# A decoder layer on one core: the cross attention's mask moves from TensorE products to a VectorE add, with norms and self values in other slots

## The chip, the core and the metric

The kernel runs on one core of one Trainium2 chip. The metric is the time of one execution in device microseconds (us); the figure for a kernel is the median of its runs. Five engines work beside each other: TensorE (PE in the profile: matrix products, with its weight loads shown apart as PEld), VectorE (DVE), ScalarE (ACT), GpSimd (POOL) and SyncE (SP, which here only issues DMAs).

## What is computed

One decoder layer with norms after each residual sum, for 32 sequences of 256 tokens, 256 features, float32 in and out. Cut to what matters:

```python
x = layernorm(x + self_attention(x))        # 16 heads of 64, 4 kv heads, rotary, ALiBi bias
x = layernorm(x + cross_attention(x, ctx))  # 16 heads of 16, windows of 64 tokens
x = layernorm(x + ffn(x))                   # 256 -> 1024 (gate, up) -> 256, quantized weights
# inside cross_attention, per head:
p = einsum(q, k) / sqrt(16)
p = where(mask, p, finfo.min)               # causal, own and previous window, same cell id
a = softmax(p); o = einsum(a, v)
```

The cross attention's mask depends on the token's cell id, so it is made anew for every sequence; all 16 heads share it.

## The kernel before, in words

**Tiles and stages.** One sequence (a "batch" b) is the unit. Its 256 query tokens are two tiles of 128. Self attention is cut into 8 units of a batch (a query tile, a pair of kv heads and two of their groups: four heads), cross attention into 4 units (a query tile and 8 of 16 heads: two halves of four heads each). A unit's scores go to two PSUM banks of 128x512 float32 (one "half" each).

**Order.** TensorE, VectorE and ScalarE run in an order written out by hand: the loop at the end of the kernel goes through slots, two to a step, and emits the instructions of each slot one function after the other. GpSimd and SyncE are placed by the framework's scheduler. Each engine works through its own queue in order. In step n (part 0, then part 1):

- part 0: `self_turn(n-1)` transposes the probabilities of the unit before (L452, into bank t, copied to pT by ScalarE, L457); then the cross attention's pieces, then `self_scores(n)`: products (L396), ALiBi product (L406), row maximum by VectorE (nm, L417), exponentials by ScalarE (p, L423).
- part 1: `self_normal(n)` scales p by the reciprocal row sums on VectorE (rinv L437, p L440); in even steps `self_values` multiplies pT with v (L469) and ScalarE copies the result (oT, L476).
- in odd steps `cross_mask` (part 0, ahead of the self scores) and `cross_scores` (after them) run, in part 1 the exponentials of the first half; the second half's exponentials, the transposes of the cross probabilities (xt, L688), the values (xo, L704) and the transposing back (xr, L724) follow in the next two steps.
- the rest are generators, which do one piece in a slot and then `yield` the number of slots to the next: `self_inputs` (projections, L333, of the next batch), `self_output` (wo, L484), `cross_inputs` (norm of the context zc, its transposes zcT, keys L594, values L606, the mask's tile), `cross_output` (norm of the attention output zo, transposes zoT, product xw L750, residual sum L754, norm of x2) and `feed_forward` (ff L797, gu L812 and L818, ffm L824, gu L833 on GpSimd, hib L836, hiT L843, ffo L849).

**Cross scores before.** `cross_mask` takes two banks (`xs`) and starts each with one bfloat16 product of an identity with the mask tile, repeated over four heads (L643, 128x512): so the bank holds 0 or a large negative number. `cross_scores` accumulates the scores onto it (L657), VectorE takes the row maxima from the bank (xnm, L666), and ScalarE computes the exponentials out of the bank into the SBUF tile xp (L679). The two banks stay taken from the mask product until the last exponential. All eight PSUM banks come from one pool.

**Norms.** A norm is: statistics on VectorE (L180, L181), reciprocal root on GpSimd in three small operations (`rstd_of`, L187 to L189), scaling on ScalarE (`scaled`, L201). Where the scaling stands in a list named `last`, it is emitted when that list is emptied: ahead of the self scores in part 0, and at the end of a slot.

**Eight steps are one period**: in steady state one batch enters and one leaves in 8 steps. I number them 0 to 7: step 0 is the one of a batch's first self unit. Cross scores fall in steps 1, 3, 5 and 7, self values in 0, 2, 4 and 6.

Of the kernel before, what the change touches and what calls it, by code (L numbers as in the profile page):

```python
# [10 lines left out]
BF16 = mybir.dt.bfloat16  # L11
# [39 lines left out]
def kernel(  # L51
# [159 lines left out]
    def prepare_cross():  # L211


        nc.sync.dma_start(vecs_sb, vecs)
        nc.sync.dma_start(cols_sb, cols)
        for j, (w, dst) in enumerate(
            (
                (wxk, xkv_w[:, :, 0:D]),
                (wxv, xkv_w[:, :, D : 2 * D]),
                (wxq, xq_w),  # L220
                (wxo, xo_w),
            )
        ):
            raw = work("tr", [P, NDC, D], 3)
            nc.sync.dma_start(raw, w.rearrange("(c p) n -> p c n", p=P))
            for dc in range(NDC):
                nc.gpsimd.tensor_scalar(
                    dst[:, dc, :], raw[:, dc, :], vecs_sb[:, j, 0, dc : dc + 1], None, ALU.mult
                )
            if j == 0:  # L230
                nc.sync.dma_start(wo_sb, Wo.rearrange("(c p) n -> p c n", p=P))
            if j in xbias:
                more = work("xp", [P, 512])
                row = more[:, 0:D]
                nc.sync.dma_start(row, rows[j].partition_broadcast(P))
                for dc in range(NDC):
                    nc.gpsimd.tensor_scalar(
                        more[:, D + dc * P : D + (dc + 1) * P],
                        ones,
                        vecs_sb[:, j, 1, dc : dc + 1],  # L240
                        None,
                        ALU.mult,
                    )
            yield 2
            pb = bank("mm")
            if j in xbias:
                for dc in range(NDC):
                    nc.tensor.matmul(
                        pb[:, 0:D],
                        more[:, D + dc * P : D + (dc + 1) * P],  # L250
                        raw[:, dc, :],
                        start=(dc == 0),
                        stop=(dc == NDC - 1),
                    )
                nc.vector.tensor_tensor(xbias[j], pb[:, 0:D], row, ALU.add)
            else:
                for ch in range(NDC):
                    for dc in range(NDC):
                        nc.tensor.matmul(
                            pb[:, ch : ch + 1],  # L260
                            raw[:, dc, ch * P : (ch + 1) * P],
                            vecs_sb[:, j, 1, dc : dc + 1],
                            start=(dc == 0),
                            stop=(dc == NDC - 1),
                        )
                nc.vector.tensor_tensor(xbcol[j], pb[:, 0:NDC], cols_sb[:, j, :], ALU.add)
            yield 2
# [291 lines left out]
    def cross_inputs(b):  # L559
# [12 lines left out]
            last.append(partial(scaled, zc[:, t, :], cs[:, t, :], rstds[t]))  # L572
        ck = work("ck", [P, L], 1)
        nc.gpsimd.tensor_copy(ck, ck_i)
        yield
        zcT = work("tr", [P, NDC, L], 3)
        for t in range(NT):
            transposed(zcT[:, :, t * P : (t + 1) * P], zc[:, t, :], "zcT")


        eq = work("eq", [P, NT, P], 1)
        s["mask"] = mask = work("mask", [P, NT, P], 2, BF16)
        for rows_, t, k0 in ((slice(0, P), 0, 0), (slice(0, 64), 1, 64), (slice(64, P), 1, 128)):
            nc.gpsimd.tensor_scalar(
                eq[rows_, t, :], ck[rows_, k0 : k0 + P], cq_sb[rows_, b, t : t + 1], BIG, ALU.is_equal, ALU.mult
# [49 lines left out]

    spans = {0: ((0, P, 0, 0),), 1: ((0, 64, 64, NT), (64, P, P, 1))}

    def cross_mask(b, i):
        s = state[b]
        qc, ch = cross_units[i]  # L640
        s["xs", i] = banks = [bank("xs") for _ in range(2)]
        for half in range(2):
            nc.tensor.matmul(  # L643
                banks[half].rearrange("p (h k) -> p h k", k=P),
                ident_b,
                s["mask"][:, qc, :].unsqueeze(1).to_broadcast([P, XHH, P]),
                start=True,
                stop=False,
            )

    def cross_scores(b, i):
        s = state[b]
        qc, ch = cross_units[i]
        for q0, q1, k0, _t in spans[qc]:
            for half in range(2):
                rows_ = slice(half * 64, (half + 1) * 64)
                nc.tensor.matmul(  # L657
                    s["xs", i][half].rearrange("p (h k) -> p h k", k=P)[q0:q1],
                    s["xqT", qc][rows_, ch, q0:q1],
                    kTz[rows_, ch, :, k0 : k0 + P],  # L660
                    start=False,
                    stop=True,
                )
        s["xnm", i] = [small("xnm", 4) for half in range(2)]
        for half in range(2):
            nc.vector.tensor_reduce(  # L666
                s["xnm", i][half],
                s["xs", i][half].rearrange("p (h k) -> p h k", k=P),
                AX.X,
                ALU.max,  # L670
                negate=True,
            )

    def cross_exp(b, i, half):
        s = state[b]
        s["xp", i, half] = p = work("xp", [P, 512])
        for j in range(XHH):
            cols = slice(j * P, (j + 1) * P)
            nc.scalar.activation(  # L679
                p[:, cols], s["xs", i][half][:, cols], AF.Exp, bias=s["xnm", i][half][:, j : j + 1]  # L680
            )

    def cross_turn(b, i, half):
# [53 lines left out]
    def cross_output(b, t):  # L737
        s = state[b]
        on = s["on", t]
        mv = stats(on, "zo")  # L740
        rstd = rstd_of(mv, "zo")
        yield
        last.append(partial(scaled, on, on, rstd))
        yield 2
        zoT = work("zT", [P, NDC, P])
        transposed(zoT, on, "zoT")
        yield
        py = bank("xw")
        for dc in range(NDC):
            nc.tensor.matmul(py[:, 0:D], zoT[:, dc, :], xo_w[:, dc, :], start=(dc == 0), stop=(dc == NDC - 1))  # L750
        if t == 0:
            s["x2"] = work("x2", [P, NT, D])
        h = s["x2"][:, t, :]
        nc.vector.tensor_tensor(h, py[:, 0:D], s["x1", t], ALU.add)  # L754
        mv = stats(h, "x2")
        rstd = rstd_of(mv, "x2")
        yield
        scaled(h, h, rstd)


    def feed_forward(b):
# [112 lines left out]
    for b in range(B):  # L874
        s0 = 16 * b
        if b:
            at(s0 - 16, self_inputs(b))
        at(s0 + 3, cross_inputs(b))
        for t in range(NT):
            at(s0 + 2 * (5 + 4 * t), self_output(b, t))  # L880
            at(s0 + 2 * (CROSS + 5 + 4 * t) + 1, cross_output(b, t))
        at(s0 + 2 * (CROSS + 11) + 2, feed_forward(b))

    with tc.manual_schedule(engines={mybir.EngineType.PE, mybir.EngineType.DVE, mybir.EngineType.Activation}):
        running = []
        slot = min(starts)
        while starts or running:
            step, part = divmod(slot, 2)
            k, odd = divmod(step - CROSS, 2)
            for gen in starts.pop(slot, ()):  # L890
                running.append([slot, gen])

            def cross(f, unit, *more):
                if 0 <= unit < 4 * B:
                    f(*divmod(unit, 4), *more)

            def own(f, unit):
                if 0 <= unit < 8 * B:
                    f(*divmod(unit, 8))


            if part == 1:
                own(self_normal, step)
            if part == 1 and not odd:
                cross(cross_exp, k, 0)
            if part == 0 and odd:
                cross(cross_exp, k, 1)
            for r in list(running):
                if r[0] == slot:
                    wait = next(r[1], r)  # L910
                    if wait is r:
                        running.remove(r)
                    else:
                        r[0] += wait or 1
            if part == 0:
                own(self_turn, step - 1)
                if odd:
                    cross(cross_back, k - 1)
                    cross(cross_turn, k, 0)
                else:  # L920
                    cross(cross_turn, k - 1, 1)
                    cross(cross_mask, k)
                flush()
                own(self_scores, step)
                if not odd:
                    cross(cross_scores, k)
            else:
                if step % 2 == 0 and 0 <= step // 2 - 1 < 4 * B:
                    self_values(*divmod(step // 2 - 1, 4))
                if not odd:  # L930
                    cross(cross_values, k - 1)
            flush()
            slot += 1
# [95 lines left out]
```

## Time and profile before

| What | us |
|---|---|
| median of three runs (lowest, highest) | 2486.79 (2483.45, 2487.99) |
| the profiled execution | 2485.1 |
| its span, from the first to the last instruction | 2483.3 |
| TensorE busy in the span | 2362.9 |
| VectorE busy | 1947.5 |
| ScalarE busy | 1710.2 |
| GpSimd busy | 1117.4 |

The profile is of one execution. It gives for each group of instructions (a line of the kernel, an engine, the tiles written and read) the count, the busy time, the mean duration in ns, and the idle time of the engine just ahead of it with what ended it. The timeline lists instructions in order of time. "In 74.07 us a batch" below is the distance at which the timeline repeats itself: the transposes zoT ahead of a step 0 start at 1202.57 and at 1276.64 on TensorE.

### The profile page before, as it was taken

What the parts mean: (1) busy time and instruction counts of PE and PEld (TensorE: products, weight loads), DVE (VectorE), ACT (ScalarE), POOL (GpSimd) and SP (SyncE); (2) the same over time, 40 slices, a digit from 0 to 9 for tenths busy, and PEclk for the clock granted to TensorE, in tenths of its full rate; (3) what the DMA queues carried; (4) which work ended last, traced back from release to release, by engine and by line L of the source; (5) the groups of instructions that cost most, each with busy time, mean ns of one, the idle gap of its engine ahead of it and who ended that gap; (6) DMA issues with size and microseconds to landing.
All of it is one profiled execution on the core that took longest, in us unless ns stands there. A gap on an engine that the chain in (4) does not pass through costs nothing.

```text
span 2483.3 us, 52717 instructions
## 1 busy us (share of the span) xinstructions
PE 2362.9 (95%) x17956; PEld 1689.6 (68%) x17956; DVE 1947.5 (78%) x4773; ACT 1710.2 (69%) x5057; POOL 1117.4 (45%) x1855
## 2 busy tenths in 40 slices
PE   6999999999999999999999999999999999999985
PEld 4766776776777666777666777676776666777653
DVE  4867877877777887877887878887887887878865
ACT  2566766766767766767766767766767766767763
POOL 6244444444444444444444444444444444444432
PEclk9999999999999999999999999999999999999996
DMA  5211211111111121121111121111211111111000
GB/s 177 79 46 44 53 51 46 41 45 48 52 53 46 35 50 48 50 54 46 36 49 48 52 53 46 37 49 48 52 52 46 36 50 46 51 48 37 22 21 9
DMA packets 104824, 121.09 MB, mean 49 GB/s; under 512 B 21734, under 2 KB 74854, under 8 KB 104556
## 3 DMA queue, kind: packets, MB, share of 16 engines
q1 hardware_dynamic: 103424, 115.96, 17.6%
q8 instruction: 143, 2.34, 0.4%
q10 hardware_dynamic: 1132, 1.76, 0.2%
q14 instruction: 125, 1.02, 0.1%
HBM read 37.69 MB, written 8.39 MB: 19 GB/s over the span
## 4 chain that ended last, share of the span: by engine, by line
PE 63%; DVE 17%; POOL 7%; ACT 7%; DMA 3%; issue 2%; SPq 1%; POOLq 0%; ACTq 0%; DVEq 0%
PE proj L333 10%; PE s L396 9%; PE t L452 6%; PE o L469 5%; PE wo L484 5%; DVE p L440 4%; ACT p L423 4%; DVE nm L417 3%; PE xs L657 3%; PE xt L688 3%; PE ff L797 3%; PE xv L606 2%; PE xk L594 2%; PE v L365 2%; DVE gu L812 2%
## 5 line engine op out<-in xcount | busy, mean ns | idle before, releaser
L423 ACT ACTIVATE p<-s,nm 128x256 f32<-128x256 f32 x1024 | 471.8, 474 | 190.4 <-DVE nm L417 188.1
L417 DVE TENSOR_REDUCE nm<-s 128x2 f32<-128x512 f32 x512 | 329.0, 684 | 189.0 <-PE s L406 170.3
L440 DVE TENSOR_SCALAR p<-p,rinv 128x256 f32<-128x256 f32 x1024 | 454.0, 485 | 18.1
L457 ACT COPY pT<-t 128x512 f32<-128x512 f32 x512 | 285.3, 629 | 84.4 <-PE t L452 80.6
L396 PE MATMUL s<-kT,qT 64*128 64x256 f32 x2048 | 313.4, 406 | 6.8 <-DVE gu L812 6.3
L679 ACT ACTIVATE xp<-xs,xnm 128x128 f32<-128x128 f32 x1024 | 303.0, 416 | 5.2 <-DVE xnm L666 5.2
L452 PE MATMUL t<-ident,p 128*128 128x128 f32 x2048 | 272.5, 275 | 8.1 <-DVE p L440 7.7
L452 PEld LDWEIGHTS t<-ident,p 128*128 128x128 f32 x2048 | 236.1, 141 | 34.4 <-DVE p L440 5.7
L396 PEld LDWEIGHTS s<-kT,qT 64*128 64x128 f32 x2048 | 186.2, 187 | 105.5 <-DVE gu L812 29.1
L333 PE MATMUL proj<-xT,wq_sb 128*128 128x256 f32 x1024 | 254.7, 392 | 0.0
L469 PE MATMUL o<-pT,v 128*64 128x256 f32 x2048 | 252.7, 389 | 0.0
L484 PE MATMUL wo<-wo_sb,oT 128*128 128x256 f32 x1024 | 250.2, 387 | 0.0
L357 POOL TENSOR_TENSOR qT<-qT,other 128x512 f32<-128x512 f32 x128 | 164.6, 1286 | 184.5 <-DMA other<-psin 143.7
L484 PEld LDWEIGHTS wo<-wo_sb,oT 128*128 128x128 f32 x1024 | 190.3, 191 | 60.1 <-issue 36.6
L333 PEld LDWEIGHTS proj<-xT,wq_sb 128*128 128x128 f32 x1024 | 185.8, 191 | 46.3 <-issue 25.7
L555 POOL TENSOR_TENSOR qb<-qb,rx_sb 128x256 f32<-128x256 f32 (+1 forms) x96 | 87.3, 910 | 275.5 <-DMA other<-qb 266.7
L423 ACT ACTIVATION_READ_ACCUMULATOR p<-s,nm 128x1 f32 x1024 | 210.1, 205 | 0.0
L469 PEld LDWEIGHTS o<-pT,v 128*64 128x64 f32 x2048 | 136.8, 138 | 89.1 <-issue 24.1
L201 ACT ACTIVATE x<-x,rstd_x 128x256 f32<-128x256 f32 x64 | 38.3, 598 | 194.6 <-DVE ffm L824 177.3
L666 DVE TENSOR_REDUCE xnm<-xs 128x4 f32<-128x512 f32 x256 | 163.8, 681 | 3.4 <-PE xs L657 3.4
L690 ACT COPY xpT<-xt 128x512 f32<-128x512 f32 x256 | 164.0, 641 | 1.4 <-ACT pT L457 0.3
L342 DVE TENSOR_TENSOR psin<-proj,rs_sb 128x512 f32<-128x512 f32 x160 | 110.6, 691 | 55.6 <-PE proj L333 49.8
(159 smaller groups left out, 4646.7 us busy)
## 6 DMA issues: line engine op xcount, KB each, us to landing
other<-psin SPq DMA_DIRECT2D x640, 64.0 KB, 2.0
xT<-in_xt_dram SPq DMA_DIRECT2D x32, 256.0 KB, 2.8
xs<-in_x_dram SPq DMA_DIRECT2D x32, 256.0 KB, 2.8
cs<-in_ctx_dram SPq DMA_DIRECT2D x32, 256.0 KB, 2.9
other<-qb SPq DMA_DIRECT2D x64, 128.0 KB, 2.0
kTz<-tr SPq DMA_DIRECT2D x256, 32.0 KB, 2.0
other<-qb SPq DMA_DIRECT2D x128, 64.0 KB, 1.9
out_dram<-y SPq DMA_DIRECT2D x32, 256.0 KB, 2.3
```

The costliest lines, as they stand in the source:

```text
L333: nc.tensor.matmul(pq[:, c * L : (c + 1) * L], w[:, dc, c * P : (c + 1) * P], xT[:, dc, :], start=(dc == 0), stop=(dc == NDC - 1),)
L357: nc.gpsimd.tensor_tensor(d2, d2, other, ALU.add)
L396: nc.tensor.matmul(banks[half][:, rr * L : (rr + 1) * L], qT[rows_, rr, qc * P : (qc + 1) * P], kT[rows_, kc, :], start=(rr == 0), stop=False,
L417: nc.vector.tensor_reduce(nm, banks[half].rearrange("p (h k) -> p h k", k=L), AX.X, ALU.max, negate=True)
L423: nc.scalar.activation(p[:, cols], banks[half][:, cols], AF.Exp, bias=nm[:, rr : rr + 1], accum_out=sums[:, rr : rr + 1],)
L440: nc.vector.tensor_scalar(p[:, cols], p[:, cols], rinv[:, rr : rr + 1], None, ALU.mult)
L452: nc.tensor.transpose(pt[:, j * P : (j + 1) * P], p[half][:, rr * L + kk * P : rr * L + (kk + 1) * P], ident,)
L457: nc.scalar.copy(pT[half], pt)
L469: nc.tensor.matmul(po[half * HD : (half + 1) * HD, rp * L : (rp + 1) * L], s["v"][:, kk, (2 * kc + half) * HD : (2 * kc + half + 1) * HD], ...
L484: nc.tensor.matmul(py[:, 0:D], s["oT", qc, kc][:, r, :], wo_sb[:, 4 * kc + r, :], start=(kc == 0 and r == 0), stop=(kc == 1 and r == 3),)
L679: nc.scalar.activation(p[:, cols], s["xs", i][half][:, cols], AF.Exp, bias=s["xnm", i][half][:, j : j + 1])
L690: nc.scalar.copy(pT, pt)
```

## The change

Three things are changed.

1. `cross_mask` and its two products are gone. `cross_scores` takes its banks after the self scores, its products start the banks themselves (`start=True`), and VectorE then adds the mask (now float32 instead of bfloat16) to each bank and writes the sum to the SBUF tile xp. Row maxima are taken from xp, and the exponentials work in place in xp. xp has 4 buffers instead of 2.
2. Norms' slots: `cross_inputs` starts one slot earlier and waits one slot more between its scaling and its transposes; in `cross_output` the transposes and all after them come one slot earlier, and the last scaling goes into `last`, so that it stands at the end of its slot.
3. `self_values` moves from part 1 of an even step, where it stood behind the generators' pieces, to part 0, directly behind the self scores.

```diff
@@ prepare_cross
-                more = work("xp", [P, 512])
+                more = work("xp", [P, 512], 4)
@@ cross_inputs (its start: at(s0 + 3, ...) becomes at(s0 + 2, ...))
         nc.gpsimd.tensor_copy(ck, ck_i)
-        yield
+        yield 2
         zcT = work("tr", [P, NDC, L], 3)
...
-        s["mask"] = mask = work("mask", [P, NT, P], 2, BF16)
+        s["mask"] = mask = work("mask", [P, NT, P])
@@
-    def cross_mask(b, i):
-        s = state[b]
-        qc, ch = cross_units[i]
-        s["xs", i] = banks = [bank("xs") for _ in range(2)]
-        for half in range(2):
-            nc.tensor.matmul(
-                banks[half].rearrange("p (h k) -> p h k", k=P),
-                ident_b,
-                s["mask"][:, qc, :].unsqueeze(1).to_broadcast([P, XHH, P]),
-                start=True,
-                stop=False,
-            )
-
     def cross_scores(b, i):
         s = state[b]
         qc, ch = cross_units[i]
+        banks = [bank("xs") for _ in range(2)]
         for q0, q1, k0, _t in spans[qc]:
...
-                    start=False,
+                    start=True,
                     stop=True,
                 )
+        for half in range(2):
+            s["xp", i, half] = p = work("xp", [P, 512], 4)
+            nc.vector.tensor_tensor(
+                p.rearrange("p (h k) -> p h k", k=P),
+                banks[half].rearrange("p (h k) -> p h k", k=P),
+                s["mask"][:, qc, :].unsqueeze(1).to_broadcast([P, XHH, P]),
+                ALU.add,
+            )
         s["xnm", i] = [small("xnm", 4) for half in range(2)]
         for half in range(2):
             nc.vector.tensor_reduce(
                 s["xnm", i][half],
-                s["xs", i][half].rearrange("p (h k) -> p h k", k=P),
+                s["xp", i, half].rearrange("p (h k) -> p h k", k=P),
@@ cross_exp
-        s["xp", i, half] = p = work("xp", [P, 512])
+        p = s["xp", i, half]
...
-                p[:, cols], s["xs", i][half][:, cols], AF.Exp, bias=s["xnm", i][half][:, j : j + 1]
+                p[:, cols], p[:, cols], AF.Exp, bias=s["xnm", i][half][:, j : j + 1]
@@ cross_output
         last.append(partial(scaled, on, on, rstd))
-        yield 2
+        yield
         zoT = work("zT", [P, NDC, P])
...
-        scaled(h, h, rstd)
+        last.append(partial(scaled, h, h, rstd))
@@ the loop over the slots
                     cross(cross_turn, k - 1, 1)
-                    cross(cross_mask, k)
                 flush()
                 own(self_scores, step)
                 if not odd:
                     cross(cross_scores, k)
-            else:
                 if step % 2 == 0 and 0 <= step // 2 - 1 < 4 * B:
                     self_values(*divmod(step // 2 - 1, 4))
+            else:
                 if not odd:
                     cross(cross_values, k - 1)
```

In the changed program's written order, the statistics of zc stand in VectorE's queue ahead of step 3's nm (they stood at that step's end), the product xw stands in TensorE's queue ahead of the next step's transposes t (it stood behind the next step's self scores), and on GpSimd the reciprocal root of the first x2 tile stands ahead of the rotation of the cross queries (qb, other, xqT, L555 to L557). On SyncE the load of the cell ids stands behind the copies into kTz and the copies of qb instead of ahead of them.

More of the change, by code (lines that the diff above doesn't have):

```diff
@@ L657, in cross_scores @@
                 nc.tensor.matmul(
-                    s["xs", i][half].rearrange("p (h k) -> p h k", k=P)[q0:q1],
+                    banks[half].rearrange("p (h k) -> p h k", k=P)[q0:q1],
                     s["xqT", qc][rows_, ch, q0:q1],
                     kTz[rows_, ch, :, k0 : k0 + P],
-                    start=False,
+                    start=True,
                     stop=True,
                 )
+        for half in range(2):
[6 more added lines that the diff above has]
+            )
         s["xnm", i] = [small("xnm", 4) for half in range(2)]
@@ L877 @@
             at(s0 - 16, self_inputs(b))
-        at(s0 + 3, cross_inputs(b))
+        at(s0 + 2, cross_inputs(b))
         for t in range(NT):
```

## The prediction

> **What bounds the kernel now.** First the page: busy shares and the chain of work that ended last.
>
> ```profile
> PE 2362.9 (95%) x17956; PEld 1689.6 (68%) x17956; DVE 1947.5 (78%) x4773; ACT 1710.2 (69%) x5057; POOL 1117.4 (45%) x1855
> ...
> PE 63%; DVE 17%; POOL 7%; ACT 7%; DMA 3%; issue 2%; SPq 1%; POOLq 0%; ACTq 0%; DVEq 0%
> ```
>
> TensorE is busy 95% and carries most of the chain, but 17% of it is VectorE: some stretch of a period runs at VectorE's pace or near it. Next the windows of one steady batch and the next, 74.07 us each (columns: stretch, length, then busy us of PE, PEld, DVE, ACT, POOL).
>
> ```profile
> 1202.57:1276.64 74.07, 72.52 (x562) 52.21 (x561) 60.22 (x149) 53.36 (x160) 34.48 (x57) 1.00 0.18 47
> 1276.64:1350.71 74.07, 72.31 (x561) 52.13 (x560) 59.70 (x148) 53.03 (x159) 34.30 (x57) 1.00 0.18 47
> ```
>
> TensorE leaves under 2 us in a batch, VectorE some 14 us. Where VectorE has no slack its timeline shows, here from step 7 to step 1 (start, length, instruction, idle before it and what ended it):
>
> ```profile
> 1272.44 1.29 DVE L417 TENSOR_REDUCE nm<-s 128x2 f32<-128x512 f32 x2 [0.66 <-PE s L396]
> 1273.65 1.29 DVE L666 TENSOR_REDUCE xnm<-xs 128x4 f32<-128x512 f32 x2
> ...
> 1276.44 2.47 DVE L818 TENSOR_TENSOR gu<-gu,ff 128x512 f32<-128x512 f32 x4
> ...
> 1280.07 1.29 DVE L417 TENSOR_REDUCE nm<-s 128x2 f32<-128x512 f32 x2 [0.72 <-PE s L406]
> ...
> 1283.49 1.21 DVE L824 TENSOR_REDUCE ffm<-gu 128x1 f32<-128x1024 f32 x1
> ...
> 1287.87 0.69 DVE L836 TENSOR_SCALAR hib<-gu 128x1024 bf16<-128x1024 f32 x1 [1.34 <-POOL gu L833]
> ...
> 1290.43 1.28 DVE L417 TENSOR_REDUCE nm<-s 128x2 f32<-128x512 f32 x2
> ```
>
> In step 1 the self scores start at 1286.58 on TensorE, but nm comes 3.8 us later, without idle time: VectorE is still at the feed-forward's maxima. I call step 7's nm to step 1's transposes t "stretch A" (21.3 to 22.2 us from batch to batch, 21.7 in the mean) and the other 52.9 us "stretch B". B is TensorE's: the last p (L440) there lies ahead of the transposes that need it by 1.3 to 5 us (medians over the batches, end of L440 to the start of L452), but for step 6, where it is just in time. In A the slack is 1.4 us (step 0), 0.3 (step 1) and 0.9 (step 7).
>
> [...] L342 (a bank times an SBUF table) has a mean of 691 ns and L818 679. [...] no exponential out of SBUF is in this trace[...]. [...] L440 takes 0.62 us alone and 1.83 beside the rotation's L357; the add has one input in PSUM, and L754, of that kind, takes 0.41 with GpSimd at work. [...] the trace shows some 0.09 us at each, as from xt to s in every step.
>
> **Part 1, mask products away, adds in.** TensorE loses 256 products. A pair costs less than two means of 379 ns, since products overlap; the chain has it whole:
>
> ```profile
> 1231.27 0.43 PE xs L643 x2
> ```
>
> Four pairs a batch: 4 x 0.43 = 1.7 us (128 pairs: 55 us), on the path wherever TensorE is the bound. VectorE gains two adds in each odd step. Back to back such operations start 0.61 us apart (L342 and L349, 1239.37 and 1239.98), so 1.2 us a step, 4.9 a batch, 156 us in all. The maxima out of SBUF cost the same (L765, out of SBUF, 0.69 us; L666 0.68). [...] The banks come free after the adds, not after the exponentials: nothing gets worse, and step 7's scores, which wait 0.28 us for a bank that gu (L812) frees, take another.
>
> The adds stand ahead of xnm and p, so step n+1's transposes need p 1.2 us later. In steps 3 and 5 the slack of 1.4 and 2.5 us covers that: nothing. In steps 7 and 1 it doesn't.
>
> **Part 2, the norms.** Step 4's context transposes now wait for the scaling on ScalarE, which waits for GpSimd's roots:
>
> ```profile
>   PEld zcT L207: 60.9, 64
>   PE zcT L207: 37.5, 63
> ```
>
> Two waits a batch; in the timeline TensorE starts them at 1241.81 and 1242.70 where 1241.16 and 1242.03 would do: 0.65 + 0.67 = 1.3 us a batch. With statistics and scaling one slot (some 4 us) earlier the wait goes; next late is nothing near, as step 4's p has 5 us of slack. The context's load moves a slot ahead too, in SP's queue still behind the output's store; its 2.9 us have 4 slots. The x2 scaling that ScalarE sat 5.6 us on (L201, before 1215.14) moves behind other work; TensorE loses at it 0.5 us in step 1 (xo on xpT). xw, 0.89 us, now stands ahead of t: its input zT is ScalarE's, behind the exponentials of the first cross half and qb. In step 7: nm + 1.3 + 1.2 + 0.65 to xnm's first half, then 1.2 (exponentials) + 0.5 (qb) + 0.4 (zT) = nm + 5.3, while TensorE is there at nm + 4.2. That hides in A, whose VectorE is later still; in step 3 both are at nm + 5.3 (0 to 0.3 lost). Its sum and statistics (1.1 us of VectorE) leave step 0's end for a place ahead of step 0's nm. On GpSimd the roots go ahead of the query rotation; the cell ids' load no longer holds back kTz's eight copies and qb's behind them, so xqT is some 2 us earlier.
>
> **Part 3, self values.** Same 16 products, 1.9 us. Behind the scores they save one change of mode, 0.09 x 4 = 0.4 us a batch (0 to 0.4). They need pT, copied while t to s run (1.6 + 1.3 us), free by 0.1 us or more. ScalarE's oT now precedes the generators' copies: no one waits.
>
> **The sum, a batch.** Stretch A is VectorE's, from row to row:
> - nm of step 7 to nm of step 0: to L818 4.0 + 1.2, L818 2.4, x sum and statistics 1.1, xrinv and on 0.5: 9.2 (before 7.6).
> - to nm of step 1: ffm starts at +3.4, ffhup ends at +5.3, GpSimd's gu (L833) 1.1 and a handover 0.1, from hib to nm 2.6: 9.1 (before 10.3: the x sum is gone, and gu no longer waits for the rotation).
> - to the transposes: p's second half was done at +4.0, now +5.2; they can start 0.44 earlier: 4.8 (before 3.8).
>
> A: 23.1 against 21.7, **1.4 longer**, although TensorE has less to do in it; TensorE waits some 2 us for p in step 1. **Stretch B**: three of the four masks (steps 3, 5, 7) 1.3, zcT 1.3, three mode changes 0.3, step 7's bank 0.4: **3.3 shorter**; less 0.5 for small lateness (zT in step 3, pT in step 2, xib in step 5, p beside GpSimd's rotation in step 0, each 0 to 0.3). Net 3.3 - 0.5 - 1.4 = 1.4 us a batch. 29 of the 32 batches are in steady state: 41 us. In the first batches VectorE also has the weights' quantization, and the last 100 us are a chain of waits in which four adds cost 4.9 and masks and earlier slots give as much back: 0. So 2485.1 - 41 = 2444 for the profiled execution. The median lies 1.7 above it: **2446**.
>
> **Rivals.**
> - *VectorE becomes the bound (slower).* Its idle 14 us a batch are not free: nm waits for scores, rinv for exponentials, hib for GpSimd. If these waits recur, every odd step is longer by its adds less its mask, 4 x (1.2 - 0.43) = 3.1, A's waits add 0.5 and the zcT gain of 1.3 is all that is left: +2.3 x 29 = 65, some 2550. It decides from the point where steps 3 and 5 have less than 1.2 us of slack. For it: step 1 is there already. Against: 1.4 and 2.5 us were measured in steps 3 and 5. Chance 0.16.
> - *A eats all.* If p beside the rotation in step 0 and a late xw make A longer by 2.8 instead of 1.4: 2485. For it: p pairs of 1.83 us exist. Chance 0.14.
> - *TensorE stays the bound throughout.* If A's waits close up (GpSimd's gu under other work), the whole 1.7 + 1.3 + 0.4 + 0.4 = 3.8 is gained: 29 x 3.8 = 110, 2377. Against: VectorE's row in A has no idle left to give but hib's. Chance 0.08.
> - The change surely does what it says: the order lists no L643.
>
> **How the numbers follow.** Forecast 0.62, own range 2420 to 2472. A measurement of this kernel can tell 0.2%, 5 us, from no change. The second rival spreads over 2472 to 2500, half of it within 5 us; faster is the forecast, the third rival and a little over a third of the second: 0.75; same 0.08; slower 0.17. With both ends of the unknown costs [...] and 2 in 10 left out at the far ends, the range is 2400 to 2500.
>
> **What would show it.** The zcT waits gone; in step 1 TensorE waiting 1 to 3 us for p (L440), the largest wait of TensorE; nm to nm 9.2 and 9.1 in A; adds of 0.69 us each; steps 3 and 5 without a wait for p; a batch of some 72.7 us. Waits for p in steps 3 and 5 would make me wrong to the slow side, none in step 1 to the fast side.

## The result, and the profile after

| | before | after |
|---|---|---|
| median of four runs (lowest, highest), us | 2487.39 (2483.45, 2490.45) | 2455.78 (2451.57, 2457.01) |
| ratio, 95% interval | 1 | 0.9871 (0.9852 to 0.9889) |
| profiled execution and its span, us | 2485.1, 2483.3 | 2456.15, 2454.2 |
| a batch in steady state, us (mean of 27) | 74.61 | 73.42 |
| stretch A in it, us | 21.72 | 22.91 |
| stretch B in it, us | 52.89 | 50.51 |

The change gains 31.6 us, 1.3%; 2446 was forecast. Behind the cross scores, line numbers of the kernel after lie four below those of before: xw L746, gu L814 and L829, hib L832. First the page of the kernel after: busy shares, the chain of work that ended last, and the groups of the cross scores (line, engine, output and inputs, count, then busy us and mean ns, then idle time before and its cause).

```profile
PE 2299.4 (94%) x17700; PEld 1673.7 (68%) x17700; DVE 2057.2 (84%) x5029; ACT 1748.7 (71%) x5057; POOL 1104.1 (45%) x1855
...
PE 59%; DVE 28%; ACT 7%; POOL 3%; issue 2%; DMA 1%; SPq 0%; ACTq 0%; POOLq 0%; DVEq 0%
```

```profile
L675 ACT ACTIVATE xp<-xp,xnm 128x128 f32<-128x128 f32 x1024 | 327.3, 394 | 63.5 <-DVE xnm L662 63.5
L654 DVE TENSOR_TENSOR xp<-xs,mask 128x512 f32<-128x512 f32 x256 | 163.5, 679 | 1.1 <-PE xs L645 0.6 <-ACT xpT L686 0.5
L662 DVE TENSOR_REDUCE xnm<-xp 128x4 f32<-128x512 f32 x256 | 162.2, 674 | 0.0
```

TensorE has 63.5 us less to do, but the span is only 29.1 shorter. VectorE's share of the chain went from 17% to 28%: stretch A has grown. TensorE's waits for other engines tell where (line that waited, what it waited for, sum in us, times, longest):

```profile
PE t L452 <- DVE p L440: 61.1, 38, 3.4
PE xw L746 <- ACT zT L208: 38.0, 36, 2.3
```

Before, the first sum was 7.7 us and TensorE's largest wait was the 37.5 for zcT. The zcT wait has gone; in its place TensorE waits twice in stretch A of every batch, for zT ahead of xw in step 7 and for step 1's p (it is transposed at the head of step 2). VectorE's timeline from step 7 to step 1 (start, length, instruction, idle before it and what ended it):

```profile
1257.02 1.28 DVE L417 TENSOR_REDUCE nm<-s 128x2 f32<-128x512 f32 x2
1258.22 1.28 DVE L654 TENSOR_TENSOR xp<-xs,mask 128x512 f32<-128x512 f32 x2
1259.41 1.27 DVE L662 TENSOR_REDUCE xnm<-xp 128x4 f32<-128x512 f32 x2
...
1262.15 2.46 DVE L814 TENSOR_TENSOR gu<-gu,ff 128x512 f32<-128x512 f32 x4
1264.54 0.41 DVE L750 TENSOR_TENSOR x<-xw,x 128x256 f32<-128x256 f32 x1
...
1266.19 1.29 DVE L417 TENSOR_REDUCE nm<-s 128x2 f32<-128x512 f32 x2
1268.17 1.14 DVE L440 TENSOR_SCALAR p<-p,rinv 128x256 f32<-128x256 f32 x2
...
1273.11 0.69 DVE L832 TENSOR_SCALAR hib<-gu 128x1024 bf16<-128x1024 f32 x1 [1.14 <-POOL gu L829]
...
1275.67 1.28 DVE L417 TENSOR_REDUCE nm<-s 128x2 f32<-128x512 f32 x2
```

From nm to nm 9.17 and 9.48 us, and 4.26 more to the transposes at 1279.93. The adds (a pair starts 1.19 us ahead of what follows) and the sum of xw (L750) stand in this row. In the second stretch VectorE has a hole of 1.14 us in which it waits for GpSimd's gu, while in the first, from step 7's nm to step 0's, it has none: this matters below.

### The profile page after: what moved, and what is told of

Same layout as the page of the kernel before. It is cut to its first block, busy times and chain, and to the rows that moved or that the text cites. A ratio compares the mean times of both kernels' runs of the same rounds, so it can differ in the third digit from the quotient of the medians.

```text
span 2454.2 us, 52179 instructions
## 1 busy us (share of the span) xinstructions
PE 2299.4 (94%) x17700; PEld 1673.7 (68%) x17700; DVE 2057.2 (84%) x5029; ACT 1748.7 (71%) x5057; POOL 1104.1 (45%) x1855
## 3 DMA queue, kind: packets, MB, share of 16 engines
q14 instruction: 125, 1.02, 0.1%
## 4 chain that ended last, share of the span: by engine, by line
PE 59%; DVE 28%; ACT 7%; POOL 3%; issue 2%; DMA 1%; SPq 0%; ACTq 0%; POOLq 0%; DVEq 0%
PE s L396 9%; PE proj L333 9%; PE t L452 8%; DVE p L440 6%; DVE nm L417 5%; PE o L469 5%; PE wo L484 4%; ACT p L423 4%; PE xt L684 3%; DVE xp L654 3%; DVE gu L808 3%; DVE ffm L820 3%; PE xw L746 3%; DVE xnm L662 3%; PE ffo L845 2%; PE xk L594 2%
## 5 line engine op out<-in xcount | busy, mean ns | idle before, releaser
L440 DVE TENSOR_SCALAR p<-p,rinv 128x256 f32<-128x256 f32 x1024 | 424.4, 456 | 18.1
L675 ACT ACTIVATE xp<-xp,xnm 128x128 f32<-128x128 f32 x1024 | 327.3, 394 | 63.5 <-DVE xnm L662 63.5
L457 ACT COPY pT<-t 128x512 f32<-128x512 f32 x512 | 277.0, 596 | 121.7 <-PE t L452 121.2
L452 PE MATMUL t<-ident,p 128*128 128x128 f32 x2048 | 288.7, 280 | 61.4 <-DVE p L440 61.1
L396 PE MATMUL s<-kT,qT 64*128 64x256 f32 x2048 | 304.1, 417 | 0.0
L357 POOL TENSOR_TENSOR qT<-qT,other 128x512 f32<-128x512 f32 x128 | 163.8, 1280 | 133.2 <-DMA other<-psin 62.7
L333 PEld LDWEIGHTS proj<-xT,wq_sb 128*128 128x128 f32 x1024 | 187.5, 193 | 33.1 <-issue 11.9
L654 DVE TENSOR_TENSOR xp<-xs,mask 128x512 f32<-128x512 f32 x256 | 163.5, 679 | 1.1 <-PE xs L645 0.6
L662 DVE TENSOR_REDUCE xnm<-xp 128x4 f32<-128x512 f32 x256 | 162.2, 674 | 0.0
L684 PE MATMUL xt<-ident,xp 128*128 128x128 f32 x1024 | 159.7, 281 | 0.0
L686 ACT COPY xpT<-xt 128x512 f32<-128x512 f32 x256 | 155.1, 606 | 3.4 <-PE xt L684 2.3
L829 POOL TENSOR_SCALAR gu<-gu,ffhup 128x1024 f32<-128x1024 f32 x64 | 71.8, 1123 | 177.2 <-DVE ffhup L825 177.2
```

Of the source, the lines that this page charges most:

```text
L333: nc.tensor.matmul(pq[:, c * L : (c + 1) * L], w[:, dc, c * P : (c + 1) * P], xT[:, dc, :], start=(dc == 0), stop=(dc == NDC - 1),)
L396: nc.tensor.matmul(banks[half][:, rr * L : (rr + 1) * L], qT[rows_, rr, qc * P : (qc + 1) * P], kT[rows_, kc, :], start=(rr == 0), stop=False,
L440: nc.vector.tensor_scalar(p[:, cols], p[:, cols], rinv[:, rr : rr + 1], None, ALU.mult)
L452: nc.tensor.transpose(pt[:, j * P : (j + 1) * P], p[half][:, rr * L + kk * P : rr * L + (kk + 1) * P], ident,)
L457: nc.scalar.copy(pT[half], pt)
L654: nc.vector.tensor_tensor(p.rearrange("p (h k) -> p h k", k=P), banks[half].rearrange("p (h k) -> p h k", k=P), s["mask"][:, qc, :].unsque ...
```

## The experiments

Each kernel was timed beside the kernel before on the same chip, whose median lay between 2484.7 and 2487.4. So the ratios compare on one chip, while a difference between two kernels timed on different occasions may carry those 3 us. "Parts" are those of the change. A runs from step 7's nm to the first weight load of step 1's transposes. The twelve:

| kernel | median, us | ratio to before (95%) | a batch, us | A, us |
|---|---|---|---|---|
| e1_norms: part 2 alone | 2428.9 | 0.9776 (0.9760 to 0.9792) | 72.93 | 21.26 |
| e2_mask: part 1 alone | 2504.9 | 1.0083 (1.0067 to 1.0098) | 75.07 | 21.95 |
| e3_values: part 3 alone | 2431.5 | 0.9785 (0.9771 to 0.9800) | 72.92 | 21.87 |
| e4_mixed: all, steps 1 and 7 by products | 2399.4 | 0.9658 (0.9641 to 0.9675) | 71.56 | 21.26 |
| e5_no_mask: parts 2 and 3 | 2413.5 | 0.9716 (0.9699 to 0.9734) | 72.30 | 21.26 |
| e6_inverse: all, steps 3 and 5 by products | 2478.5 | 0.9963 (0.9935 to 0.9992) | 74.18 | 22.88 |
| e7_xw_back: all, first xw in its old slot | 2402.9 | 0.9667 (0.9652 to 0.9681) | 71.78 | 21.89 |
| e8_mask_zc: part 1 and the context's slots | 2412.8 | 0.9707 (0.9692 to 0.9721) | 72.09 | 21.93 |
| e9_back_one: e7, step 1 by products | 2374.7 | 0.9544 (0.9523 to 0.9565) | 70.82 | 21.14 |
| e10_back_two: e7, steps 1 and 7 by products | 2393.3 | 0.9619 (0.9597 to 0.9641) | 71.45 | 21.15 |
| e11_zc: the context's slots alone | 2436.7 | 0.9798 (0.9779 to 0.9817) | 73.14 | 21.67 |
| e12_no_mask_xw_back: e5, first xw in its old slot | 2409.2 | 0.9690 (0.9671 to 0.9709) | 72.28 | 21.25 |

### The three parts, each alone

**e1_norms.** The kernel before with part 2's lines of the diff.

```diff
-        yield            # behind ck's copy in cross_inputs
+        yield 2
-        yield 2          # behind the scaling of on in cross_output
+        yield
-        scaled(h, h, rstd)
+        last.append(partial(scaled, h, h, rstd))
-        at(s0 + 3, cross_inputs(b))
+        at(s0 + 2, cross_inputs(b))
```

> Part 2 alone on the kernel before (norms' slots; mask still by products, self values where they were). Theory T (stretch A, from step 7's nm to step 1's transposes, is VectorE's, so the adds there cost more than the products they replace; stretch B is TensorE's): the zcT waits of 1.3 us a batch go, A loses its waits of xo but gains nothing else: 1.3 to 1.8 us a batch, 29 batches, 2487 - 38 to 52 = 2435 to 2449, so faster than the whole change (2456). Rival S (TensorE bounds everything, every part gives its own TensorE time): 38 us from the zcT waits, and then the whole change should have given over 90, which it didn't. If it is above 2460, the norms' slots are not where the gain of the whole change comes from.

Measured 2428.9: faster than the whole change, as the theory said, and by more than it said. The zcT waits are no longer among TensorE's, and A is 0.5 shorter.

**e2_mask.** The kernel before with part 1's lines of the diff alone.

```diff
-                    cross(cross_mask, k)
+            nc.vector.tensor_tensor(p, banks[half], mask, ALU.add)
```

> Part 1 alone on the kernel before (mask by VectorE's add; norms and self values where they were). T: A longer by 1.0 (adds of steps 7 and 1 less idle time), B shorter by 1.3 to 1.7: 0.3 to 0.7 us a batch, about 2467 to 2478. Rival S (TensorE bounds everything): four products' pairs of 0.43, 1.7 us a batch, 2437. Rival V (VectorE bounds every odd step): 4 x (1.2 - 0.43) = 3.1 us a batch longer, 2577.

Measured 2504.9: some 19 us slower than before, where the theory had a gain. TensorE's waits say why; first the weight load's, then the product's:

```profile
PEld zcT L207 <- ACT cs L201: 87.2, 64, 3.5
```

```profile
PE zcT L207 <- ACT cs L201: 63.5, 63, 3.0
```

Before they were 60.9 and 37.5: 26 us more in either row. The two rows show the same waits, since the product comes behind its weight load, so 26 us were added and not 52. In VectorE's queue the context's statistics stand behind step 3's p, and p stands behind the two adds. VectorE's timeline of e2 has step 3's nm at 1238.77 and the first statistics 6.11 later; in the kernel before they came 5.19 after nm (1233.01 to 1238.20). From statistics to the transposes it is 3.6 us in both, so zcT is 0.92 us later. TensorE's timeline, and the same stretch by windows (length, busy us of PE, PEld, DVE, ACT and POOL, granted clock, DMA share and GB/s):

```profile
1248.47 0.44 PE L207 MATMUL zcT<-ident,cs 128*128 128x128 f32 x2 [1.48 <-ACT cs L201]
1249.37 0.66 PE L207 MATMUL zcT<-ident,cs 128*128 128x128 f32 x2 [0.46 <-ACT cs L201]
1249.82 1.91 PE L746 MATMUL xw<-xo_w,zT 128*128 128x256 f32 x4
1251.66 2.51 PE L469 MATMUL o<-pT,v 128*64 128x256 f32 x16
```

```profile
1249.60:1253.00 3.40, 3.40 (x14) 2.08 (x15) 2.68 (x7) 2.07 (x10) 2.44 (x3) 0.52 0.63 177
1253.00:1256.40 3.40, 3.40 (x23) 2.53 (x20) 1.20 (x4) 0.59 (x1) 1.05 (x3) 1.00 0.02 4
```

The wait is 1.48 us here, and behind it TensorE runs at half clock for 3.4 us: xw takes 1.91 us instead of 1.03, o 2.51 instead of 1.95. Of the 28 steady batches 13 have it, and stretch B is 1.6 us longer in them. Before, the waits were mostly 0.4 to 0.6 us and then 0.46; the one steady batch that had it had waited 1.29, and another that waited 1.29 did not have it. So a wait of TensorE can cost more than its own length.

**e3_values.** The kernel before with `self_values` behind the self scores.

```diff
                 if not odd:
                     cross(cross_scores, k)
-            else:
                 if step % 2 == 0 and 0 <= step // 2 - 1 < 4 * B:
                     self_values(*divmod(step // 2 - 1, 4))
+            else:
```

> Part 3 alone on the kernel before (self values directly behind their step's scores). T: one change of tiling mode less in each even step, 0.09 us x 4 x 29 = 11 us, less up to that for waits on pT: 2476 to 2487. Rival: the generators' products, 1.9 us later in even steps, hold up zcT's or gu's consumers: over 2492.

Measured 2431.5: a miss by 45 us. I had counted the change of tiling mode only: in the kernel before, s (`64*128`) starts 0.53 us after the first of four xt (`128*128`); where the mask's products (`128*128` too) come next, they start 0.44 after it, 0.09 less (medians). The wait for zcT, with the same slots of the norm as before, has gone:

```profile
PE zcT L207 <- ACT cs L201: 2.3, 2, 1.8
```

The 16 products of step 4's values, 1.9 us, now stand between the scores and zcT, where TensorE used to wait: work put into the hole. So parts 2 and 3 remove the same wait, by an earlier input and by other work ahead of it, and their gains of 57 and 54 don't add up: both together (e5) gain some 71.

### What the adds cost beside the other parts

**e5_no_mask.** Parts 2 and 3 on the kernel before; the mask stays with the products.

> Parts 2 and 3 without part 1 (norms' slots and self values moved; mask by products in all four units). Each alone took the zcT waits away, so they don't add up. T: 72.9 us a batch with the norms alone, less 0.35 in step 7 (scores no longer wait for gu's bank) and up to 0.3 of mode changes: 72.3 to 72.6, about 2410 to 2420; the mask's part of the whole change then costs some 40 us on top of these two. If the mask's part were a gain there, this would be over 2456.

Measured 2413.5, 42 us faster than the whole change. With these neighbours the adds cost 42 us, though they free TensorE of 55.

**e4_mixed.** The changed kernel; in units 0 and 3 (steps 1 and 7) the mask goes into the banks by products as before, in units 1 and 2 (steps 3 and 5) it is added. The mask is bfloat16 for both.

```diff
+    BY_PRODUCT = (0, 3)
...
+        by_product = i in BY_PRODUCT
+        banks = s["xs", i] if by_product else [bank("xs") for _ in range(2)]
...
+                    start=not by_product,
...
+            if by_product:
+                s["xe", i, half] = banks[half]
+                continue
```

> The changed kernel, but units 0 and 3 of a batch (steps 1 and 7) take the mask by products again and units 1 and 2 (steps 3 and 5) by the add; the mask's tile is bfloat16 for both. T: A loses 2.4 us of VectorE and gains 0.86 of TensorE, of which it has 2.9 idle: A 21 to 21.5 instead of 22.9, B as in the changed kernel: 1.4 to 1.9 us a batch, about 2400 to 2415. Rival S (TensorE bounds everything): two pairs more, 0.86 us a batch, 2481. Rival V (every add costs): half of the adds' cost gone, 2 x 0.8 x 29, about 2410; it is told from T by e2_mask.

Measured 2399.4, at the lower edge of what was expected: 14 us faster than with no adds at all, 56 faster than with all four. A is 21.26, as in e5; in steps 3 and 5 the last p ends 1.0 and 2.0 us ahead of the first transposes (medians).

**e6_inverse.** The same with `BY_PRODUCT = (1, 2)`: adds in steps 1 and 7 alone.

> The mixed kernel the other way round: units 1 and 2 (steps 3 and 5) by products, units 0 and 3 (steps 1 and 7) by the add. T (only the adds in stretch A cost): A stays 22.9, B takes two pairs of products more, 0.86 us a batch: 2456 + 25 = 2481. Rival V (an add costs the same wherever it is): as fast as the mixed kernel, 2400 to 2411.

Measured 2478.5, with A at 22.88 as in the changed kernel. So the harm is in steps 7 and 1 and the two adds in B are a gain; the rival with VectorE as the bound everywhere falls. This kernel's twelve runs spread from 2457.2 to 2496.5 us, and the mean granted clock falls with them from 0.983 to 0.966, so that time times clock stays within 0.2% (2415 and 2412) at the two ends, as the half clock from e2 in fewer or more of the batches would have it. Its profiled execution has it in step 2 of 13 of 28 batches; they take 75.09 us in the mean, the others 73.46.

### The first tile's product, in or out of stretch A

**e7_xw_back.** The changed kernel; the first tile's zoT and xw stay in their old slots, zoT ahead of step 0's scores and xw behind them.

```diff
-        yield
+        yield 2 if t == 0 else 1
```

> The changed kernel, but the first tile's zoT and xw in their old slots (zoT ahead of step 0's scores, xw behind them). T: TensorE's wait of 1.2 us for zT at the end of step 7 goes, and xw's sum and statistics (1.1 us of VectorE) leave the row to step 0's nm for the gap in which VectorE waits for gu: A 21.8 to 22.3 instead of 22.9, 17 to 32 us, 2424 to 2439. Rival (that wait lies beside VectorE's row, and the sum only changes places): 2450 to 2460.

Measured 2402.9: the theory's sign, about twice its size. VectorE's timeline of e7, with the sum of xw now in step 0:

```profile
1237.14 1.21 DVE L820 TENSOR_REDUCE ffm<-gu 128x1 f32<-128x1024 f32 x1
...
1238.96 0.20 DVE L827 TENSOR_SCALAR ffd<-ffsh,sc_down 128x1 f32<-128x1 f32 x1
1239.08 0.41 DVE L750 TENSOR_TENSOR x<-xw,x 128x256 f32<-128x256 f32 x1
1239.53 0.43 DVE L180 BATCH_NORM_STATS2 st<-x 128x6 f32<-128x256 f32 x1
1239.99 0.18 DVE L181 BATCH_NORM_AGGREGATE mv_x<-st 128x2 f32<-128x6 f32 x1
1240.30 0.69 DVE L832 TENSOR_SCALAR hib<-gu 128x1024 bf16<-128x1024 f32 x1
```

Here the sum and the statistics fill the hole in which VectorE waits for GpSimd's gu: they cost nothing. In the changed kernel they stand where VectorE is late, and the hole stays empty (the 1.14 us at hib above). nm7 to nm0 is 7.97 instead of 9.17, nm0 to nm1 9.68 instead of 9.50: A is 1.0 us shorter. TensorE's wait for zT is down to 4.5 us in all, and its wait for step 1's p to this:

```profile
1247.12 1.44 PE L452 MATMUL t<-ident,p 128*128 128x128 f32 x8 [1.10 <-DVE p L440]
```

The rest of the gain is in step 2. From its transposes to step 3's are 10.25 us in every steady batch of e7 and in 16 of 28 of the changed kernel, but 11.8 to 11.9 in the other 12, and stretch B of these is 1.7 us longer as a whole (51.51 against 49.82). A's 1.0 us in each of some 29 batches and these 12 times 1.7 make up some 50 of the 53 us. TensorE there, first a batch with it, then the one behind it without:

```profile
1205.76 1.44 PE L452 MATMUL t<-ident,p 128*128 128x128 f32 x8 [1.70 <-DVE p L440]
1207.25 0.94 PE L684 MATMUL xt<-ident,xp 128*128 128x128 f32 x4
1208.13 2.08 PE L396 MATMUL s<-kT,qT 64*128 64x256 f32 x8
```

```profile
1279.93 1.44 PE L452 MATMUL t<-ident,p 128*128 128x128 f32 x8 [1.68 <-DVE p L440]
1281.43 0.60 PE L684 MATMUL xt<-ident,xp 128*128 128x128 f32 x4
1281.96 1.14 PE L396 MATMUL s<-kT,qT 64*128 64x256 f32 x8
```

In the traces before and after all stretches of half clock start at whole multiples of 3.413 us from one another (after, 1207.36, 1354.13 and 1500.91 lie 43 steps apart). The windows of the changed kernel are cut along these steps, two of each batch; the wait of the first batch lies within one window, that of the second over the border of two.

```profile
1203.95:1207.36 3.41, 1.71 (x12) 1.30 (x12) 3.34 (x11) 2.96 (x12) 0.00 (x0) 1.00 0.00 0
1207.36:1210.78 3.42, 3.42 (x17) 1.99 (x17) 3.01 (x9) 2.89 (x5) 1.54 (x4) 0.50 0.34 96
1275.63:1279.04 3.41, 2.62 (x37) 1.97 (x26) 3.41 (x7) 2.21 (x9) 1.12 (x1) 1.00 0.00 0
1279.04:1282.46 3.42, 2.53 (x18) 2.03 (x20) 3.25 (x12) 3.42 (x11) 0.00 (x0) 1.00 0.02 5
```

TensorE is busy for 1.71 of 3.41 us in the window ahead of the half clock, and for 2.62 and 2.53 in the two that share the other wait. Behind the first the granted clock is 0.50 over 3.42 us, behind the other two it stays at 1.00 (1282.46 to 1285.87). In e7's 28 steady batches, with waits of mostly 0.7 to 1.2 us, the half clock never came.

**e12_no_mask_xw_back.** The same line in e5: no adds, first xw in its old slot.

> Parts 2 and 3 without the mask's adds, and the first tile's output product in its old slots: the fourth corner of a square with the changed kernel (2456), that with the product in its old slots (2403) and that without adds (2413). Theory I (the early output product and the adds hurt only together): within 6 us of 2413, 2407 to 2419. Rival E (the early product costs 53 us by itself): 2355 to 2366.

Measured 2409.2. The square of medians, us:

| | four adds | no adds |
|---|---|---|
| first xw in the new slot | 2455.8 | 2413.5 |
| first xw in its old slot | 2402.9 | 2409.2 |

The early product costs 53 us with the adds and 4 without; the adds cost 42 with the early product and gain 6 without. Neither is bad by itself. Why the early product is almost free without adds, VectorE's hole at hib shows, first in e5 and then in e12, and last GpSimd's queue in e12 ahead of that hole:

```profile
1247.86 0.69 DVE L836 TENSOR_SCALAR hib<-gu 128x1024 bf16<-128x1024 f32 x1 [1.82 <-POOL gu L833]
```

```profile
1251.34 0.70 DVE L836 TENSOR_SCALAR hib<-gu 128x1024 bf16<-128x1024 f32 x1 [2.11 <-POOL gu L833]
```

```profile
1247.99 0.73 POOL L555 TENSOR_TENSOR qb<-qb,rx_sb 128x256 f32<-128x256 f32 x1 [9.29 <-DMA other<-qb]
...
1250.19 1.12 POOL L833 TENSOR_SCALAR gu<-gu,ffhup 128x1024 f32<-128x1024 f32 x1
```

Without the adds the rotation comes late, as its DMA does, and holds gu back; VectorE waits 1.8 or 2.1 us here (medians 1.5 and 1.4) wherever the x sum stands, and A is 21.3 in both. With the adds the rotation is over in time (1269.16 in the changed kernel, gu at 1271.96), A follows VectorE's own row, and each 1.0 us in that row counts. The DMA is early there because of SyncE's order, first in e12 and then in the changed kernel (step 7's nm at 1235.13 and 1257.02):

```profile
1238.73 0.35 SPq L565 DMA_DIRECT2D ck_i<-in_cell_k_dram  x1
1239.17 6.06 SPq L630 DMA_DIRECT2D kTz<-tr  x8
```

```profile
1257.60 5.15 SPq L630 DMA_DIRECT2D kTz<-tr  x8
...
1264.12 1.04 SPq L565 DMA_DIRECT2D ck_i<-in_cell_k_dram  x1
```

Where the cell ids' load stands ahead of the copies into kTz, these start 3.7 to 4.0 us behind step 7's nm, otherwise 0.6 to 0.7 (medians). The scheduler has put the load behind in the six kernels with adds in step 7 (the changed one, e2, e6, e7, e8, e9), and ahead in the other eight. So "the adds" of the square are the adds with this order; no run has one without the other.

**e10_back_two.** e7 with `BY_PRODUCT = (0, 3)`, so adds in steps 3 and 5 alone.

> As the one before, with the masks of steps 1 and 7 by products, adds in steps 3 and 5 alone. Beside the mixed kernel (2399) it differs by the first tile's output product in its old slots only. Theory I (the early output product hurts only together with the adds of steps 7 and 1, because all three fill VectorE's stretch A): the same within 6 us, 2393 to 2405. Rival E (the early output product costs what it cost with four adds, 53 us, by itself): 2346 to 2365.

Measured 2393.3, 6 from the 2399.4 of e4: the same statement without the adds of steps 7 and 1, and again no 53 us.

**e9_back_one.** e7 with `BY_PRODUCT = (0,)`: step 1's mask by products, step 7's by adds.

> The changed kernel with the first tile's output product in its old slots, and the mask of step 1's unit by products again, so that only steps 3, 5 and 7 have adds. Theory T (what is left of the add's harm is TensorE's wait for p in step 1, 1.1 us, after adds that stand ahead of it in VectorE's queue): that wait goes, for 0.43 us of products, -0.67 a batch, 2380 to 2392. Rival (TensorE's wait there only moves to step 2 or 7, since VectorE is late throughout stretch A): no faster than with all four adds, 2398 to 2408.

Measured 2374.7, 5 us below the expectation and the fastest here, 4.6% (4.4 to 4.8) below the kernel before. TensorE's t of step 1 in its timeline has no wait, and its largest wait is this:

```profile
PE t L452 <- DVE p L440: 13.0, 14, 2.5
```

A batch is 0.96 us shorter than in e7: 0.75 in A, 0.2 in B. It also beats e10 by 19 us, so step 7's adds, with the order of SyncE that comes with them, are a gain once xw is out of their way (in e12, without them, VectorE still waits 0.82 us for the scores ahead of step 0's nm). Only step 1's are a loss.

### The context's slots

**e8_mask_zc.** e2 with the context norm's slots of part 2 alone.

```diff
-        yield            # behind ck's copy in cross_inputs
+        yield 2
-        at(s0 + 3, cross_inputs(b))
+        at(s0 + 2, cross_inputs(b))
```

> Part 1 plus, of part 2, only the context's norm (starts one slot earlier, two slots between scaling and transposes); zo, x2 and self values as before. The mask alone was 19 us slower. Theory Z: its adds in step 3 push zc's statistics back, which stand behind p in VectorE's queue, and so lengthen TensorE's waits at zcT from 1.3 to 2.1 us a batch; with the statistics ahead of them both go: 2505 - 2.1 x 29 = 2444. Rival: the 19 us are the adds in stretch A and in step 7; then only the old wait of 1.3 goes: 2467.

Measured 2412.8, 92 us below e2 and 31 below the theory's 2444. So the slower time of the mask alone was the zcT wait and the half clock behind it; zcT is no longer among TensorE's waits.

**e11_zc.** The same two lines on the kernel before.

> The kernel before with the context norm's slots alone moved. Theory T: the two waits of 0.65 us for zcT go, 1.3 to 1.6 us a batch, 2440 to 2450; the mask's adds on top of that then bring -27 to -37 (2413 was measured), so that they are a gain once the context's statistics stand ahead of them in VectorE's queue. Rival: the context's slot alone gives all of it, 2410 to 2418, and the adds nothing.

Measured 2436.7, a little below the expectation: these two lines are 51 of the 57 us of part 2. On top of them the adds gain 24 us (e8). By the profiles B is then 51.47 before the adds and 50.16 after: 1.31 us, as predicted for three masks, and A grows by 0.26.

## Why the prediction was right, and where it was off

The time was within 10 us of the forecast and the way was the right one: A longer, B shorter, TensorE's largest wait that for step 1's p. That it came so near is in part luck: the half clock of step 2, in none of the steps, costs some 20 us (12 batches, 1.7 us each), and without it the time would be about 2436 by that estimate. The "some 72.7 us" a batch came from a single batch of 74.07; from the mean of 74.61 the forecast is 73.2, and 73.42 was measured. By its steps:

| term, us a batch | predicted | measured |
|---|---|---|
| nm7 to nm0 | 9.2 | 9.17 |
| nm0 to nm1 | 9.1 | 9.50 |
| nm1 to the transposes | 4.8 | 4.23 |
| A | +1.4 | +1.19 |
| B | -2.8 net | -2.38 |
| both | -1.4 | -1.19 |

- **nm7 to nm0** was read from VectorE's row, term by term, and held.
- **nm0 to nm1** is 0.4 longer than predicted: p's first pair takes 1.14 us instead of 0.62 beside GpSimd's three rotations (L555 to L557, 1266.93 to 1269.16). Before, a pair took 0.62 us with nothing of GpSimd beside it, 1.39 beside L357 and 1.83 beside L357 and L557 (medians). That lateness was named, but booked in B and at most 0.3. The hole of 1.14 us at hib is the 1.1 for gu that the term has in it.
- **nm1 to the transposes** is 0.6 shorter: they start when the first of p's four operations is done, 4.1 us after nm, and then wait only shortly for the others (eight transposes in 1.44 us instead of 1.04).
- **"That hides in A"**, of xw's wait in step 7: true of TensorE's wait (1.06 us at 1262.22, while VectorE is at gu until 1264.54 and comes to nm without idle time). What failed is its sum and statistics, "1.1 us of VectorE", counted as leaving one term for the other: "the x sum is gone" from nm0 to nm1. They left the hole at hib, where they cost nothing, for a row without a hole: 1.20 us more there, 0.18 back (e7 against the changed kernel). The total of A was right, but the step hid what this one slot costs: 53 us, more than the whole change gains. Some 30 of them are A's 1.0 us a batch; some 20 are the half clock in step 2, since the longer row makes TensorE's wait for step 1's p 1.7 us instead of 0.7 to 1.2.
- **B** falls short by 0.42. In twelve of 28 batches step 2 runs at half clock for a while, and B is 51.51 us in these and 49.82 in the other sixteen: 0.7 a batch, more than the whole of it. In batches without it B is 3.1 shorter, nearer to the 3.3 before the 0.5 for small lateness was taken off. That a wait in A would be paid again in B was in none of the steps.
- **Masks 1.3 in B**: e8 against e11 has 1.31. **Mode changes 0.3**: e5 against e1, part 3 where the zcT wait has already gone, has 15 us, but 6.8 of them are the wait of step 7's scores for gu's bank, which is gone in e5; what is left is 0.3 a batch. **Step 7's bank 0.4**: 6.8 us over 27 waits in e1, so 0.25 a batch, and part 3 alone (e3) ends it as part 1 alone (e2) does. **zcT 1.3**: e11 alone has 1.47 in the period. So each was right for its place in the sum, and none for a part alone.
- **xqT 2 us earlier** was booked with the norms. The order of SyncE that does it is in e2 (part 1 alone) and not in e1 (part 2 alone); qb's DMA is issued 5.9 us behind step 7's nm instead of 9.1, so 3.3 earlier.
- **Adds in steps 3 and 5 covered**: right (e4, e6). The slack of 1.4 and 2.5 us is 1.1 and 2.2 when it is taken from the end of the last p to the first transposes. So taken it is still 1.1 in step 3 after the change, where the second tile's xw now stands ahead of the transposes, and 0.1 in e8, where it does not.
- **Adds 0.69 each, maxima out of SBUF the same**: 0.679 and 0.674. **Exponentials**: the mean duration fell, 416 to 394 ns, but they overlap, and from start to start it is 296 ns instead of 252, 0.044 more. The trace before had no exponential out of SBUF, so what these would cost was not shown ahead of the change. A group's mean was the wrong row for this; the timeline's four in 1.28 us instead of 1.16 shows it.
- **The ends at nothing**: the kernel after is 3.2 us later at its first scores already and 3.3 at the fourth batch's, and the last 161 us are equal. Why the start is later stays open; no run tried it.
- **Rivals.** VectorE as the bound everywhere fell: steps 3 and 5 don't wait. "A eats all" named the two right places, p beside the rotation and a late xw, but A grew by 1.2, not 2.8. The third, TensorE the bound throughout at 2377, isn't this kernel, but e9 shows that its time was to be had, with three of the four masks added and xw in its old slot.

What the sum could not show is that the parts act on each other: -57 (norms), -54 (values) and +19 (mask) give -92 if added, and the change gives -32. Parts 2 and 3 remove one wait, and the early xw and the adds lengthen one row of VectorE.

## What to carry to other kernels

Ask of each moved piece whether it leaves a hole or a full stretch of its engine's queue, and where it arrives: the same 1.1 us of VectorE cost nothing in a hole and, with the adds beside it and the half clock that followed, 53 us of the kernel in a full stretch. When an operation goes from the bounding engine to a second one, do it only in the steps where that engine's result has slack; here the adds in steps 3, 5 and 7 gained and those in step 1 lost. Price a wait of TensorE like the 1.7 us here with what comes behind it; look whether an edit has also moved what the scheduler places; and try parts apart before you take or leave a change whole.

## What was not expected of the hardware

TensorE's clock fell to half for 3.41 us after waits of about 1.48 and 0.46 us within 1.4 us (13 of 28 batches of part 1 alone) and after single ones of 1.67 to 1.88 us (12 of 28 batches of the changed kernel) and of about 1.66 (13 of 28 of e6), but in none of e7's 28, whose waits were mostly 0.7 to 1.2. One such fall makes a batch 1.6 to 1.7 us longer here. At equal waits the place in the steps of 3.413 us tells the two kinds of batch apart in all 28 of the changed kernel: the wait for step 1's p began 0.07 to 0.75 us behind a border in the 12 batches with a fall and 1.02 to 3.26 in the 16 without. Each of these 12 falls ended a window in which TensorE had been busy for 1.53 to 1.74 of 3.41 us, about half. Three more windows of this trace in steady state (from 248.22, 688.54 and 1791.04) had as little, 1.73 or 1.74 us; why they had no fall stays open, and no run moved the steps.

In e6 a batch with a fall takes 75.09 us in the mean, which is 22 of these steps, so the next wait would meet the same place. Whether its times spread by 39 us from run to run for this reason, by how early a run comes to that place, was not shown; only one of its runs left a trace.
